# Another order for the first phase of a layer-norm, block-sparse and LoRA gate kernel: two tiles transposed ahead of the first product

## The chip, the cores and the metric

The kernel runs on one core of a Trainium2 chip. The metric is the device time of one execution in microseconds; the median of three runs is given. Five engines run their own instruction streams: TensorE (PE, matrix products and transposes; its weight loads are listed apart as PEld), VectorE (DVE), ScalarE (ACT), GpSimd (POOL) and SyncE (SP), which here only issues DMAs. The profile is one execution that the hardware profiler recorded.

## The reference

The input x has 2 batches of 1024 tokens with 1024 features. Each token is layer-normed, goes through a block-sparse linear layer (a 32 x 32 block of the weight counts if its mask has a nonzero entry) and through a linear layer with eight low-rank experts, whose mixing coefficients come from the mean token of the batch.

```python
def block_sparse(data, mask, weight, bias):
    bm = mask.reshape(Nb, 32, Kb, 32).sum(axis=(1, 3)) > 0
    wb = weight.reshape(Nb, 32, Kb, 32) * bm[:, None, :, None]
    return jnp.einsum('bsk,nk->bsn', data, wb.reshape(N, K)) + bias

def lora(x, W_org, lora_down, lora_up, lora_keys, Wq):
    base = jnp.einsum('bsi,oi->bso', x, W_org)
    q = jnp.einsum('bi,ki->bk', x.mean(axis=1), Wq)
    coeffs = softmax(jnp.einsum('bk,ek->be', q, lora_keys) / sqrt(128))
    h = jnp.einsum('bsi,eir->bser', x, lora_down)
    return base + jnp.einsum('be,bser,ero->bso', coeffs, h, lora_up)

xn = layernorm(x)
out = x + block_sparse(xn, ...) * silu(lora(xn, ...))
```

## The kernel before

Every product of two float32 matrices is made of three products: each factor is split into a high part (a copy rounded to the type that TensorE takes in one pass, written by ScalarE) and a low part (what the rounding left, a subtraction on VectorE or GpSimd), and hi x hi, hi x lo and lo x hi are summed in PSUM. So each tile of weights or of tokens costs one cast and one subtraction, and TensorE waits for both.

The first phase is the block-sparse product of batch 0 (1024 tokens in eight tiles of 128, numbered 0 to 7) with the first 512 output features. Everything from line 652 on is in a written order: TensorE, VectorE, ScalarE and GpSimd each execute their instructions in the order in which the program lists them. SP's order of DMA issues is not written out by hand; the DMAs are issued ahead, as buffers come free.

Tokens come in two ways. Tiles 0 to 3 are loaded as they lie (x_load) and go through x_stats (two halves of batch-norm statistics on VectorE), rstd_of (aggregate and add on VectorE, a power on GpSimd), shift_of (VectorE), x_norm_half (ScalarE, half a tile), x_turn (four 128 x 128 transposes on TensorE for a half), x_hi (ScalarE) and x_lo (VectorE). Tiles 4 to 7 come already transposed from a second copy of x, eight chunks of 128 features: xprep loads a chunk, subtracts the tokens' means (spread over all partitions by spread_means, four transposes on TensorE) and casts it; xprep_lo makes the low part. Their scale is applied when the result is evacuated. Tiles 4 to 7 are also loaded as they lie, because the mean token needs them normed: statistics by x_stats (tiles 4 and 5) or on ScalarE by mean_sum and square_sum with mean_of and rstd_from (6 and 7), then x_norm.

The weights' first 512 columns come in two quarters of 256. For each quarter the mask is summed over its blocks (mask_sum, on VectorE or ScalarE), mask_join and mask_spread make a small matrix of it, mask_apply_mm spreads it with eight small products on TensorE, mask_apply_cp copies it for GpSimd, and w_mul multiplies the weights (VectorE reads the mask in PSUM, GpSimd the copy). w_hi and w_lo split them. The second argument of w_mul, w_hi and w_lo is the first of the chunks of 128 features, two at a time where nothing else is said.

The products: p0 to p3 with t0 to t3 are the first quarter for token tiles 0 to 3, q0 to q3 with u0 to u3 the second quarter, q4 to q7 with u4 to u7 both quarters at once for tiles 4 to 7. t0(2, 4) issues the three products of chunks 2 and 3. PSUM has four banks for them, so q1, q0, q2, q3, and then tiles 4 to 7, need a bank whose former result has been evacuated (quarter_evac, tile_evac, on VectorE).

warm_up(n) issues n products of constants whose result nobody reads. They stand where TensorE would be idle; keep_busy issues some of them inside t0.

The mean token: add_acc adds the normed tiles up in the tile 0 buffer (1024 columns on VectorE or GpSimd); halves splits the sum, query takes its mean over the tokens with four products and multiplies by Wq, scores and soft make the coefficients, scale_up scales the up-projection. y_prep loads and splits chunks of the down-projection, and y_mul(0, 0, 0) is the first product of the next phase. The staging buffers of xprep, y_prep and scale_up are six of one pool.

The lines that matter: x_stats 611 (instruction at 150), rstd_of 152, shift_of 161, x_norm_half 644 (168), x_turn 599 (211), x_hi 602, x_lo 605 (607), mask_sum 250, w_mul 584 (588), w_hi 590, w_lo 593 (595), the products 457, 460 and 461, warm_up 672 (674), xprep 225, xprep_lo 235 (238), add_acc 648 (650), halves 333 (338, 339), query 342 (348 to 357), quarter_evac 484 (473), y_prep 405 (412, 413). Line 1394 is the product of the last phase, 1148 of the one before it.

Of the kernel before, what the change touches and what calls it, by code (L numbers as in the profile page):

```python
# [22 lines left out]
NH = 512  # L23
# [5 lines left out]
NWARM2 = 12  # L29
# [3 lines left out]
def kernel(  # L33
# [618 lines left out]
    with tc.manual_schedule(engines={mybir.EngineType.PE, mybir.EngineType.DVE, mybir.EngineType.Activation, mybir.EngineType.Pool}):  # L652
# [25 lines left out]
        warm_up(NWARM)  # L678
        x_stats(0, 0)
        x_stats(0, 1)  # L680
        rstd_of(0)
        shift_of(0)
        x_norm_half(0, 0)
        x_norm_half(0, 1)
        x_turn(0, 0)
        x_turn(0, 1)
        warm_up(NWARM2)
        x_stats(1, 0)
        x_stats(1, 1)
        rstd_of(1)  # L690
        mask_sum(0, 0, mh[0][:, 0, :], nc.vector)
        x_hi(0, 0)
        mask_sum(0, 1, mh[0][:, 1, NH:], nc.scalar, 1)
# [3 lines left out]
        shift_of(1)  # L697
        mask_apply_mm(0)
        warm_up(4)
        x_hi(0, 1)  # L700
        mask_apply_cp(0, 0, 4, nc.scalar.copy)
        w_mul(0, 0, nc.vector, 1)
        w_mul(0, 1, nc.vector, 1)
        w_mul(0, 2, nc.gpsimd)
        w_hi(0, 0, 1)
        w_hi(0, 1, 1)
        x_lo(0, 0)
        x_norm_half(1, 0)
        w_hi(0, 2)
        w_lo(0, 0, nc.vector, 1)  # L710
        w_lo(0, 1, nc.vector, 1)
        p0, t0 = open_gemm(0, 0, s0, 0, NQ)
        p1, t1 = open_gemm(0, 1, s0, 0, NQ)

        keep_busy = lambda kt: warm_up((4, 1, 2, 0)[kt])
        t0(0, 1, keep_busy)
        x_turn(1, 0)
        t0(1, 2, keep_busy)
        x_hi(1, 0)
        mask_apply_cp(0, 4, 8, nc.scalar.copy)  # L720
        w_lo(0, 2)
        t0(2, 4, keep_busy)
        x_lo(1, 0)
        w_mul(0, 4, nc.vector)
        w_mul(0, 6, nc.gpsimd)
        x_norm_half(1, 1)
        w_hi(0, 4)
        t1(0, 3)
        x_turn(1, 1)
        x_lo(0, 1)  # L730
        w_hi(0, 6)
        w_lo(0, 4)
        x_hi(1, 1)
        t1(3, 4)
        t0(4, 6)
        w_lo(0, 6, nc.gpsimd)
        x_stats(2, 0)
        x_stats(2, 1)
        rstd_of(2)
        mask_sum(1, 0, mh[1][:, 0, :], nc.scalar)  # L740
        t0(6, 8)
        x_lo(1, 1)
        shift_of(2)
        x_norm_half(2, 0)
        x_norm_half(2, 1)
        x_stats(3, 0)
        x_stats(3, 1)
        rstd_of(3)
        add_acc(1, nc.gpsimd)
        t1(4, 7)  # L750
        x_turn(2, 0)
        t1(7, 8)
        x_hi(2, 0)
        x_turn(2, 1)
        x_lo(2, 0)
        shift_of(3)
        x_hi(2, 1)
        x_norm_half(3, 0)
        x_norm_half(3, 1)
        x_lo(2, 1)  # L760
        mask_sum(1, 1, mh[1][:, 1, :], nc.vector)
        mask_spread(1)
        p2, t2 = open_gemm(0, 2, s0, 0, NQ)
        t2(0, 4)
        x_turn(3, 0)
        x_hi(3, 0)
        t2(4, 5)
        mask_apply_mm(1)
        mask_apply_cp(1, copy=nc.scalar.copy)
        w_mul(1, 4, nc.gpsimd)  # L770
        w_mul(1, 6, nc.gpsimd)
        x_lo(3, 0)
        x_turn(3, 1)
        t2(5, 8)
        w_mul(1, 0, nc.vector)
        x_hi(3, 1)
        x_lo(3, 1)
        w_hi(1, 0)
        w_mul(1, 2, nc.vector)
        p3, t3 = open_gemm(0, 3, s0, 0, NQ)  # L780
        t3(0, 8)
        w_hi(1, 2)
        w_hi(1, 4)
        w_hi(1, 6)
        w_lo(1, 0)
        quarter_evac(0, 0, p0)
        w_lo(1, 2)
        mean_sum(6)
        mean_sum(7)
        w_lo(1, 4)  # L790
        w_lo(1, 6)
        quarter_evac(1, 0, p1)
        x_stats(4, 0)
        x_stats(4, 1)
        x_stats(5, 0)
        rstd_of(4)
        x_stats(5, 1)
        q0, u0 = open_gemm(0, 0, s0, NQ, NQ)
        u0(0, 8)
        shift_of(4)  # L800
        x_norm(4)
        rstd_of(5)
        mean_of(6)
        mean_of(7)
        q1, u1 = open_gemm(0, 1, s0, NQ, NQ)
        u1(0, 6)
        spread_means(0, 1)
        u1(6, 8)
        quarter_evac(2, 0, p2)
        xprep(0, 1, 0)  # L810
        xprep(0, 1, 1)
        shift_of(5)
        x_norm(5)
        xprep_lo(0, 1, 0)
        quarter_evac(3, 0, p3)
        q2, u2 = open_gemm(0, 2, s0, NQ, NQ)
# [745 lines left out]
```

## Time and profile before

| | |
|---|---|
| three runs | 438.65, 438.69, 438.95 us |
| profiled execution | 439.04 us, of which 437.3 us from the first to the last instruction (the span) |
| granted TensorE clock | 1.000 |
| instructions | 5766 |

Busy time in five stretches of the first 66 us, from the windows of the profile (us, number of instructions in brackets):

```profile
7.66:13.17 5.51, 5.31 (x32) 3.89 (x32) 4.73 (x12) 3.08 (x8) 1.42 (x2) 1.00 1.03 419
13.17:24.17 11.00, 10.65 (x75) 9.46 (x76) 9.28 (x21) 8.49 (x16) 4.58 (x6) 1.00 1.03 409
24.17:35.74 11.57, 11.57 (x105) 11.50 (x104) 10.91 (x25) 7.84 (x14) 4.38 (x5) 1.00 0.92 345
35.74:56.27 20.53, 20.53 (x121) 18.17 (x119) 19.58 (x38) 13.17 (x23) 4.40 (x5) 1.00 0.47 154
56.27:65.61 9.34, 9.34 (x43) 7.73 (x42) 6.72 (x19) 2.42 (x5) 1.66 (x1) 1.00 0.11 30
```

After the window and its length come PE, PEld, DVE, ACT and POOL, then the granted clock of TensorE, the share of the 16 DMA engines that was busy, and GB/s. The stretches are: from the first transposes to the first product; to the point from which TensorE is never idle; to spread_means; to the query; to the first y_mul. The duration of a TensorE product includes its way through the array, so products overlap and a busy share of 1 is not a measure of useful work; the distance of their starts is.

### The profile page before, as it was taken

Reading aid. Unit: us, or ns where it says so; the run is one execution under the profiler, and the core shown is the slowest. Engines: PE = TensorE matmul, PEld = TensorE weight load, DVE = VectorE, ACT = ScalarE, POOL = GpSimd, SP = SyncE. Lnnn points to the kernel's source line nnn. Section 1 sums busy time; section 2 is a strip of 40 time slices with the busy share of each in tenths; the row PEclk is TensorE's granted clock in tenths of the full one; section 3 lists DMA queues with packets and bytes.
Section 4 is the critical chain, followed back from the end, with each engine's and each line's share of the span. In section 5 each row is a group of like instructions: output and inputs, shape, how many; then the busy total and the mean of one; then the engine's idle time right before and its main releaser. Section 6 shows DMA issues by size and latency. Waiting matters only on the chain.

```text
span 437.3 us, 5766 instructions
## 1 busy us (share of the span) xinstructions
PE 429.7 (98%) x2029; PEld 358.0 (82%) x2029; DVE 305.2 (70%) x508; ACT 184.4 (42%) x312; POOL 79.0 (18%) x103
## 2 busy tenths in 40 slices
PE   7999999999999999999999999999999999999996
PEld 5899888888888888888888888788888888888885
DVE  5889977766626769879966968877647385375624
ACT  3787436354731222236334344466335233441510
POOL 3342210002220313134132130010020030002000
PEclk9999999999999999999999999999999999999999
DMA  7994607676896798984699866996282165228003
GB/s 269 413 371 152 216 25 224 234 253 208 263 296 176 244 268 298 315 327 144 191 273 295 254 191 192 348 253 206 58 210 80 48 141 151 93 54 210 26 1 121
DMA packets 44477, 88.48 MB, mean 202 GB/s; under 512 B 4624, under 2 KB 13088, under 8 KB 44448
## 3 DMA queue, kind: packets, MB, share of 16 engines
q1 hardware_dynamic: 28944, 64.77, 43.6%
q0 software_dynamic: 6624, 16.26, 16.0%
q10 hardware_dynamic: 8880, 7.08, 5.0%
q8 instruction: 16, 0.26, 0.2%
q14 instruction: 13, 0.11, 0.1%
HBM read 68.17 MB, written 19.93 MB: 201 GB/s over the span
## 4 chain that ended last, share of the span: by engine, by line
PE 90%; DMA 4%; DVE 2%; ACT 1%; issue 1%; POOL 0%; SPq 0%; DVEq 0%; ACTq 0%
PE acc_ps L1394 25%; PE acc_ps L461 12%; PE acc_ps L457 12%; PE acc_ps L460 12%; PE py L1394 10%; PE psv L1148 5%; PE psw L421 3%; PE psw L422 3%; PE psw L423 3%; PE psw L1148 2%; DMA xs<-xv 1%; DMA misc<-xv 1%; DMA raw<-xv 1%; PE warm L674 1%; DMA acc<-in_x_dram 1%
## 5 line engine op out<-in xcount | busy, mean ns | idle before, releaser
L1394 PE MATMUL acc_ps<-xw,ow 128*128 128x512 f32 (+1 forms) x492 | 112.2, 384 | 0.3 <-DVE xw L1219 0.3
L457 PE MATMUL acc_ps<-slot,xgrp 128*128 128x512 f32 (+1 forms) x288 | 106.5, 370 | 0.1
L1394 PEld LDWEIGHTS acc_ps<-xw,ow 128*128 128x128 f32 x492 | 90.8, 188 | 19.0 <-DVE xw L1219 0.7
L461 PE MATMUL acc_ps<-slot,xgrp 128*128 128x512 f32 (+1 forms) x288 | 105.5, 366 | 0.2 <-DVE xgrp L607 0.2
L460 PE MATMUL acc_ps<-slot,xgrp 128*128 128x512 f32 (+1 forms) x288 | 105.3, 366 | 0.1
L461 PEld LDWEIGHTS acc_ps<-slot,xgrp 128*128 128x128 f32 x288 | 54.3, 188 | 9.6 <-DVE xgrp L607 0.6
L457 PEld LDWEIGHTS acc_ps<-slot,xgrp 128*128 128x128 f32 x288 | 54.3, 188 | 9.3 <-ACT slot L591 0.6
L460 PEld LDWEIGHTS acc_ps<-slot,xgrp 128*128 128x128 f32 x288 | 54.3, 189 | 8.9 <-POOL slot L595 0.3
L1394 PE MATMUL py<-xw,ow 128*128 128x512 f32 x192 | 46.3, 389 | 0.0
L1394 PEld LDWEIGHTS py<-xw,ow 128*128 128x128 f32 x192 | 36.0, 188 | 7.5
L1262 DVE TENSOR_TENSOR ow<-raw,ow 128x1024 fp32r<-128x1024 f32 (+1 forms) x32 | 34.7, 1088 | 9.2 <-ACT ow L1261 9.1
L1261 ACT CAST ow<-raw 128x1024 fp32r<-128x1024 f32 (+1 forms) x32 | 29.5, 941 | 2.5 <-DVE raw L1255 1.5
L509 POOL DMA_DIRECT2D stash<-in_x_dram x16 | 14.4, 902 | 72.4 <-DVE stash L506 72.4
L1377 POOL DMA_DIRECT2D gate<-in_xT_dram x12 | 10.5, 913 | 93.1 <-DVE gate L1371 67.8
L431 ACT CAST slot<-wo 128x512 fp32r<-128x512 f32 x16 | 9.9, 620 | 35.7 <-DVE wo L428 35.7
L421 PE MATMUL psw<-cut,dhi 128*128 128x512 f32 x64 | 24.9, 389 | 0.0
L422 PE MATMUL psw<-cut,dhi 128*128 128x512 f32 x64 | 24.9, 389 | 0.0
L423 PE MATMUL psw<-cut,dlo 128*128 128x512 f32 x64 | 24.9, 389 | 0.0
L1438 DVE TENSOR_TENSOR py<-py,s 128x512 f32<-128x512 f32 x8 | 5.6, 698 | 27.6 <-ACT s L1401 27.6
L1255 DVE TENSOR_TENSOR raw<-raw 128x512 f32<-128x512 f32 x32 | 21.4, 688 | 0.6
L1247 DVE TENSOR_TENSOR raw<-raw,m_sb 128x1024 f32<-128x1024 f32 x8 | 9.7, 1222 | 13.8 <-DMA raw<-in_wu_dram 13.8
L506 DVE TENSOR_TENSOR stash<-stash,mine 128x512 f32<-128x512 f32 x16 | 11.1, 692 | 10.8 <-ACT mine L482 10.6
(211 smaller groups left out, 604.6 us busy)
## 6 DMA issues: line engine op xcount, KB each, us to landing
wo<-in_worgT_dram SPq DMA_DIRECT2D x24, 256.0 KB, 3.8
raw<-in_x_dram SPq DMA_DIRECT2D x11, 512.0 KB, 4.7
ds<-in_down_dram SPq DMA_DIRECT2D x16, 256.0 KB, 3.1
stash<-in_x_dram POOLq DMA_DIRECT2D x16, 256.0 KB, 5.2
raw<-in_wu_dram SPq DMA_DIRECT2D x8, 512.0 KB, 5.4
raw<-yu SPq DMA_DIRECT2D x8, 512.0 KB, 3.7
out_dram<-stash ACTq DMA_DIRECT2D x14, 256.0 KB, 4.3
misc<-xv SPq DMA_DIRECT2D x12, 256.0 KB, 3.9
```

What stands on the lines that cost most here:

```text
L421: nc.tensor.matmul(ps, lhsT=dhi[:, c, :], rhs=u[c][:, 0, :], start=c == 0, stop=False)
L422: nc.tensor.matmul(ps, lhsT=dhi[:, c, :], rhs=u[c][:, 1, :], start=False, stop=False)
L423: nc.tensor.matmul(ps, lhsT=dlo[:, c, :], rhs=u[c][:, 0, :], start=False, stop=c == 3)
L457: nc.tensor.matmul(ps, lhsT=xs[:, kt, 0, cols], rhs=w[:, kt, 0, wc], start=kt == 0, stop=False)
L460: nc.tensor.matmul(ps, lhsT=xs[:, kt, 0, cols], rhs=w[:, kt, 1, wc], start=False, stop=False)
L461: nc.tensor.matmul(ps, lhsT=xs[:, kt, 1, cols], rhs=w[:, kt, 0, wc], start=False, stop=kt == NKT - 1)
L509: nc.gpsimd.dma_start(res, x[at], accum_op=ALU.add)
L1148: nc.tensor.matmul(ps, lhsT=w[:, a, wl, c, :], rhs=u[:, ul, :], start=start and c == 0 and n == 0, stop=c == 1 and n == 2, skip_group_chec ...
L1255: nc.vector.tensor_tensor(raw[:, o], raw[:, a], raw[:, b], op)
L1261: nc.scalar.copy(o[:, a:b, 0], raw[:, a:b])
L1262: nc.vector.tensor_tensor(o[:, a:b, 1], raw[:, a:b], o[:, a:b, 0].bitcast(F32), ALU.subtract)
L1394: nc.tensor.matmul(ps, lhsT=o[:, a, wl, j, :], rhs=xw[j][:, m, xl, cols], start=start and j == 0 and k == 0, stop=j == 3 and k == 2, skip_ ...
```

## The change

The order of the calls between the first warm_up and the loop of y_mul is another one; the functions that they call are the same. In the main:

- x_norm_half(0, 1) comes before x_norm_half(0, 0). x_turn(0, 0) and x_turn(0, 1) have warm_up(10) between them; before, they stood together with warm_up(12) after them. warm_up(4) after the mask products becomes warm_up(7), and the warm-ups inside t0 go from 4, 1 and 2 to 0, 0 and 2 (32 in all, before 36).
- x_turn(1, 0) comes before the first product t0(0, 1); x_hi(0, 1) and x_lo(0, 1) move behind w_hi(0, 6) and w_lo(0, 4).
- w_mul(0, 4) moves ahead of the low parts of the first chunks, both mask copies ahead of the first w_mul, and the statistics of tile 2 and of tiles 4 and 5 come earlier among VectorE's work. add_acc(1) on GpSimd moves ahead of w_mul(1, 4); mean_sum(7) and mean_of move behind quarter_evac(0, 0).
- u1(0, 6) runs before u0, u6(0, 4) and u5 before u4, and u7 before the last part of u6. spread_means stands after u0.
- The chunks of xprep come in the order 1, 0, 3, 5, 2, 4, 7, 6.
- add_acc(3) and add_acc(4) move up among the evacuations and xprep; before, tiles 2 to 7 were added in one row. y_prep(0, 0, 0) moves ahead of x_norm(5), before the sums are complete; tile_evac of q4, q5 and q6 moves behind scale_up.

The core of the diff:

```diff
         warm_up(NWARM)
+        keep_busy = lambda kt: warm_up((0, 0, 0, 2)[kt])
+        halves, query, scores, soft = coeffs(0)
+
         x_stats(0, 0)
+        p1, t1 = open_gemm(0, 1, s0, 0, NQ)
         x_stats(0, 1)
         rstd_of(0)
         shift_of(0)
+        x_norm_half(0, 1)
         x_norm_half(0, 0)
-        x_norm_half(0, 1)
         x_turn(0, 0)
+        x_hi(0, 0)
+        x_stats(1, 1)
+        x_stats(1, 0)
+        rstd_of(1)
+        mask_sum(0, 1, mh[0][:, 1, NH:], nc.scalar, 1)
+        mask_sum(0, 0, mh[0][:, 0, :], nc.vector)
+        warm_up(10)
         x_turn(0, 1)
-        warm_up(NWARM2)
-        x_stats(1, 0)
-        x_stats(1, 1)
-        rstd_of(1)
-        mask_sum(0, 0, mh[0][:, 0, :], nc.vector)
-        x_hi(0, 0)
-        mask_sum(0, 1, mh[0][:, 1, NH:], nc.scalar, 1)
+        p0, t0 = open_gemm(0, 0, s0, 0, NQ)
+        shift_of(1)
         mask_sum(0, 1, mh[0][:, 1, :NH], nc.vector)
         mask_join(0)
         mask_spread(0)
-        shift_of(1)
+        x_norm_half(1, 0)
         mask_apply_mm(0)
-        warm_up(4)
-        x_hi(0, 1)
         mask_apply_cp(0, 0, 4, nc.scalar.copy)
+        x_lo(0, 0)
+        mask_apply_cp(0, 4, 8, nc.scalar.copy)
         w_mul(0, 0, nc.vector, 1)
+        warm_up(7)
         w_mul(0, 1, nc.vector, 1)
+        w_mul(0, 4, nc.vector)
+        w_hi(0, 0, 1)
+        w_lo(0, 0, nc.vector, 1)
+        x_turn(1, 0)
+        w_hi(0, 1, 1)
+        w_lo(0, 1, nc.vector, 1)
+        t0(0, 1)
         w_mul(0, 2, nc.gpsimd)
-        w_hi(0, 0, 1)
-        w_hi(0, 1, 1)
-        x_lo(0, 0)
-        x_norm_half(1, 0)
         w_hi(0, 2)
-        w_lo(0, 0, nc.vector, 1)
-        w_lo(0, 1, nc.vector, 1)
-        p0, t0 = open_gemm(0, 0, s0, 0, NQ)
-        p1, t1 = open_gemm(0, 1, s0, 0, NQ)
-
-        keep_busy = lambda kt: warm_up((4, 1, 2, 0)[kt])
-        t0(0, 1, keep_busy)
-        x_turn(1, 0)
-        t0(1, 2, keep_busy)
-        x_hi(1, 0)
-        mask_apply_cp(0, 4, 8, nc.scalar.copy)
         w_lo(0, 2)
-        t0(2, 4, keep_busy)
-        x_lo(1, 0)
-        w_mul(0, 4, nc.vector)
         w_mul(0, 6, nc.gpsimd)
         x_norm_half(1, 1)
+        x_stats(2, 0)
+        x_stats(2, 1)
+        x_hi(1, 0)
+        x_lo(1, 0)
+        p2, t2 = open_gemm(0, 2, s0, 0, NQ)
+        rstd_of(2)
         w_hi(0, 4)
+        w_lo(0, 4)
+        w_hi(0, 6)
+        x_hi(0, 1)
+        x_lo(0, 1)
+        t0(1, 2)
+        t0(2, 4, keep_busy)
+        x_turn(1, 1)
+        x_hi(1, 1)
         t1(0, 3)
-        x_turn(1, 1)
-        x_lo(0, 1)
-        w_hi(0, 6)
-        w_lo(0, 4)
-        x_hi(1, 1)
         t1(3, 4)
+        shift_of(2)
+        mask_sum(1, 0, mh[1][:, 0, :], nc.scalar)
         t0(4, 6)
         w_lo(0, 6, nc.gpsimd)
-        x_stats(2, 0)
-        x_stats(2, 1)
-        rstd_of(2)
-        mask_sum(1, 0, mh[1][:, 0, :], nc.scalar)
-        t0(6, 8)
         x_lo(1, 1)
-        shift_of(2)
+        t1(4, 7)
         x_norm_half(2, 0)
+        x_turn(2, 0)
         x_norm_half(2, 1)
+        x_hi(2, 0)
         x_stats(3, 0)
         x_stats(3, 1)
         rstd_of(3)
-        add_acc(1, nc.gpsimd)
-        t1(4, 7)
-        x_turn(2, 0)
+        x_turn(2, 1)
         t1(7, 8)
-        x_hi(2, 0)
-        x_turn(2, 1)
+        x_hi(2, 1)
         x_lo(2, 0)
         shift_of(3)
-        x_hi(2, 1)
         x_norm_half(3, 0)
         x_norm_half(3, 1)
-        x_lo(2, 1)
+        t0(6, 8)
+        t2(0, 4)
+        x_turn(3, 0)
         mask_sum(1, 1, mh[1][:, 1, :], nc.vector)
         mask_spread(1)
-        p2, t2 = open_gemm(0, 2, s0, 0, NQ)
-        t2(0, 4)
-        x_turn(3, 0)
+        mask_apply_mm(1)
+        x_stats(4, 0)
+        x_lo(2, 1)
         x_hi(3, 0)
-        t2(4, 5)
-        mask_apply_mm(1)
+        x_lo(3, 0)
         mask_apply_cp(1, copy=nc.scalar.copy)
+        x_turn(3, 1)
+        x_hi(3, 1)
+        add_acc(1, nc.gpsimd)
+        quarter_evac(1, 0, p1)
+        w_mul(1, 2, nc.vector)
+        w_mul(1, 0, nc.vector)
+        w_hi(1, 0)
         w_mul(1, 4, nc.gpsimd)
         w_mul(1, 6, nc.gpsimd)
-        x_lo(3, 0)
-        x_turn(3, 1)
+        x_lo(3, 1)
+        x_stats(5, 1)
+        w_lo(1, 0)
+        w_hi(1, 2)
+        w_lo(1, 2)
+        w_hi(1, 4)
+        w_lo(1, 4)
+        w_hi(1, 6)
+        t2(4, 5)
         t2(5, 8)
-        w_mul(1, 0, nc.vector)
-        x_hi(3, 1)
-        x_lo(3, 1)
-        w_hi(1, 0)
-        w_mul(1, 2, nc.vector)
+        mean_sum(6)
         p3, t3 = open_gemm(0, 3, s0, 0, NQ)
         t3(0, 8)
-        w_hi(1, 2)
-        w_hi(1, 4)
-        w_hi(1, 6)
-        w_lo(1, 0)
+        q1, u1 = open_gemm(0, 1, s0, NQ, NQ)
+        w_lo(1, 6)
+        u1(0, 6)
         quarter_evac(0, 0, p0)
-        w_lo(1, 2)
-        mean_sum(6)
+        x_stats(5, 0)
+        rstd_of(5)
+        quarter_evac(2, 0, p2)
         mean_sum(7)
-        w_lo(1, 4)
-        w_lo(1, 6)
-        quarter_evac(1, 0, p1)
-        x_stats(4, 0)
+        mean_of(7)
+        mean_of(6)
+        square_sum(6, 0)
+        q0, u0 = open_gemm(0, 0, s0, NQ, NQ)
         x_stats(4, 1)
-        x_stats(5, 0)
+        q2, u2 = open_gemm(0, 2, s0, NQ, NQ)
         rstd_of(4)
-        x_stats(5, 1)
-        q0, u0 = open_gemm(0, 0, s0, NQ, NQ)
         u0(0, 8)
+        add_acc(3, nc.vector)
         shift_of(4)
+        quarter_evac(3, 0, p3)
+        q3, u3 = open_gemm(0, 3, s0, NQ, NQ)
+        spread_means(0, 1)
+        xprep(0, 1, 1)
+        u1(6, 8)
+        quarter_evac(1, 1, q1)
+        xprep(0, 1, 0)
+        xprep(0, 1, 3)
+        xprep_lo(0, 1, 3, nc.gpsimd)
+        square_sum(6, 1)
+        xprep_lo(0, 1, 1, nc.vector)
+        square_sum(7, 0)
+        xprep(0, 1, 5)
+        u2(0, 8)
+        xprep_lo(0, 1, 0)
+        xprep(0, 1, 2)
+        rstd_from(6)
+        square_sum(7, 1)
         x_norm(4)
-        rstd_of(5)
-        mean_of(6)
-        mean_of(7)
-        q1, u1 = open_gemm(0, 1, s0, NQ, NQ)
-        u1(0, 6)
-        spread_means(0, 1)
-        u1(6, 8)
-        quarter_evac(2, 0, p2)
-        xprep(0, 1, 0)
-        xprep(0, 1, 1)
+        quarter_evac(0, 1, q0)
+        xprep(0, 1, 4)
+        q6, u6 = open_gemm(0, 6, s0)
+        xprep_lo(0, 1, 2, nc.vector)
+        shift_of(6)
+        quarter_evac(2, 1, q2)
+        xprep(0, 1, 7)
         shift_of(5)
+        rstd_from(7)
+        xprep(0, 1, 6)
+        q4, u4 = open_gemm(0, 4, s0)
+        xprep_lo(0, 1, 6)
+        u3(0, 8)
+        u6(0, 4)
+        xprep_lo(0, 1, 4, nc.vector)
+        add_acc(4, nc.vector)
+        shift_of(7)
+        y_prep(0, 0, 0)
+        q5, u5 = open_gemm(0, 5, s0)
         x_norm(5)
-        xprep_lo(0, 1, 0)
-        quarter_evac(3, 0, p3)
-        q2, u2 = open_gemm(0, 2, s0, NQ, NQ)
-        u2(0, 8)
-        q3, u3 = open_gemm(0, 3, s0, NQ, NQ)
-        u3(0, 8)
-        for kt in range(2, 6):
-            xprep(0, 1, kt)
-            xprep_lo(0, 1, kt - 1, nc.gpsimd if kt == 4 else nc.vector)
-            if kt == 3:
-                quarter_evac(0, 1, q0)
-            square_sum(6 + (kt - 2) // 2, kt % 2)
-        xprep(0, 1, 6)
         xprep_lo(0, 1, 5, nc.gpsimd)
-        xprep(0, 1, 7)
-        rstd_from(6)
-        rstd_from(7)
-        xprep_lo(0, 1, 6)
         xprep_lo(0, 1, 7)
-        quarter_evac(1, 1, q1)
-        q4, u4 = open_gemm(0, 4, s0)
+        u5(0, 8)
+        add_acc(2, nc.vector)
+        quarter_evac(3, 1, q3)
         u4(0, 8)
-        shift_of(6)
-        shift_of(7)
+        x_norm(7)
         x_norm(6)
-        x_norm(7)
-        for i in range(2, 6):
-            add_acc(i, nc.vector)
-        quarter_evac(2, 1, q2)
+        add_acc(5, nc.vector)
         add_acc(6, nc.vector)
-        quarter_evac(3, 1, q3)
-        for h in range(2):
-            add_acc(7, nc.vector, h)
-        halves, query, scores, soft = coeffs(0)
+        add_acc(7, nc.vector, 0)
+        add_acc(7, nc.vector, 1)
         halves()
-        y00 = new_slot()
-        q5, u5 = open_gemm(0, 5, s0)
-        u5(0, 8)
-        q6, u6 = open_gemm(0, 6, s0)
-        u6(0, 4)
         query()
-        tile_evac("s", 0, 0, 4, q4)
-        y_prep(0, 0, 0)
         u6(4, 7)
+        q7, u7 = open_gemm(0, 7, s0)
         scores()
-        tile_evac("s", 0, 0, 5, q5)
         soft()
         scale_up(0, 0)
-        y_prep(0, 0, 1)
+        tile_evac("s", 0, 0, 4, q4)
+        u7(0, 8)
         u6(7, 8)
         tile_evac("s", 0, 0, 6, q6)
-        q7, u7 = open_gemm(0, 7, s0)
-        u7(0, 8)
+        y_prep(0, 0, 1)
+        tile_evac("s", 0, 0, 5, q5)
+        y00 = new_slot()
         for k in range(NKT):
             y_mul(0, 0, k)
             if k == 0:
```

More of the change, by code (lines that the diff above doesn't have):

```diff
@@ L28 @@
 NWARM = 13
-NWARM2 = 12
 @with_exitstack
```

## The prediction

> **What bounds the kernel now.** I read first the page's busy shares and the chain that ended last, then the waits of TensorE.
>
> ```profile
> PE 429.7 (98%) x2029; PEld 358.0 (82%) x2029; DVE 305.2 (70%) x508; ACT 184.4 (42%) x312; POOL 79.0 (18%) x103
> PE 90%; DMA 4%; DVE 2%; ACT 1%; issue 1%; POOL 0%; SPq 0%; DVEq 0%; ACTq 0%
> PE pt L211 <- ACT acc L168: 1.5, 1, 1.5
> PE warm L674 <- DVE ones_r L98: 1.1, 1, 1.1
> PE acc_ps L1394 <- DVE xw L1219: 0.3, 1, 0.3
> PE acc_ps L461 <- DVE xgrp L607: 0.2, 1, 0.2
> ```
>
> TensorE is the bound: after 24.17 us it waits once, 0.3 us, late in the kernel. So a microsecond won before the first y_mul product (65.61) should reach the end, as all later work hangs on TensorE's progress. The timeline of TensorE shows what can be won: matmuls without a use, and gaps.
>
> ```profile
> 1.12 4.98 PE L674 MATMUL warm<-ones_r 128*128 128x512 f32 x13 [1.12 <-DVE ones_r L98]
> 7.66 1.36 PE L211 MATMUL pt<-ident,acc 128*128 128x128 f32 x8 [1.55 <-ACT acc L168]
> 8.77 2.99 PE L674 MATMUL warm<-ones_r 128*128 128x512 f32 x12
> 11.66 0.34 PE L276 MATMUL mp<-r,misc 128*128 128x8 bf16 x8
> 11.86 1.16 PE L674 MATMUL warm<-ones_r 128*128 128x512 f32 x4
> 13.17 0.39 PE L457 MATMUL acc_ps<-slot,xgrp 128*128 128x256 f32 x1
> 13.39 1.08 PE L674 MATMUL warm<-ones_r 128*128 128x512 f32 x4
> 23.94 0.39 PE L461 MATMUL acc_ps<-slot,xgrp 128*128 128x256 f32 x1 [0.22 <-DVE xgrp L607]
> 56.27 0.39 PE L348 MATMUL mxp<-mh,inv_s 128*128 128x512 f32 x1
> ```
>
> Columns: start, time, engine, line, operation. The last line, the first query product, is my mark: both orders have issued the same useful products by then (u4, u5, half of u6 and all quarters). From 7.66 to 56.27 are 48.61 us. Starts lie 0.227 apart for a product of 512 columns, 0.1195 for 256, and about 0.38 cover a group of four transposes. Useful: 60 x 0.227 + 192 x 0.1195 + 8 x 0.38 + 0.35 (means) + 0.42 (16 mask products) = 40.4. The remaining 8.2 are 23 warm-ups (5.2) and 3.0 of gaps.
>
> The second engine is VectorE, strictly in order: it ends the last part of halves() only here.
>
> ```profile
> 11.44 0.17 DVE L266 SCALAR_TENSOR_TENSOR r<-s,pick 128x8 bf16<-128x8 f32 x1
> 12.26 0.75 DVE L588 TENSOR_TENSOR ramp<-ramp,mp 128x256 f32<-128x256 f32 x2 [0.52 <-ACT m_sb L283]
> 36.37 1.28 DVE L231 TENSOR_TENSOR xt<-xt,mean_ps 128x512 f32<-128x512 f32 x2 [0.60 <-PE mean_ps L221]
> 55.26 1.30 DVE L339 TENSOR_TENSOR ml<-acc,mh 128x512 fp32r<-128x512 f32 x2
> ```
>
> Between 11.44 and 56.56 its gaps of over 0.3 are 0.52, 0.43, 0.40, 0.60, 0.49 and 0.60: 3.04. It has little more to give than TensorE, so both chains must be worked through.
>
> **The change, step by step.** Starts on VectorE lie 0.60 apart for 512 columns, 0.33 for 256, 1.23 for a sum of 1024; ScalarE's 512-column casts 0.55 to 0.60; all from the timelines.
>
> *Start.* The halves of tile 0 are normed in the other order, so the first transposes wait for the second norm: 8.36, where before the second group stood. That is 0.70 later, hidden: ten warm-ups follow (8.78 to 11.05), then the other four transposes, and TensorE next needs the mask. On VectorE shift_of(1) (0.13) now stands ahead of the second mask sum, so the spread ends at 11.75 and the mask products start at 11.74 (before 11.60 by the weight load).
>
> *To the first product.* Both mask copies now precede the weights' multiply. Before, w_mul waited for the copy's end (12.23), not for TensorE's (12.00); so I let it wait for the second copy: 12.18 + 0.10 + 0.19 = 12.47, w_mul at 12.50 (12.40 if it waits for the first only). Then VectorE runs without a break: two w_mul (0.33 each), the w_mul of tiles 4 and 5 moved here (0.60), w_lo(0) to 14.18, w_lo(1) to 14.51, w_lo(2,3) to 15.10, two statistics of tile 2 (1.2), x_lo(1,0) 16.2 to 16.9, aggregate 0.32, w_lo(4,5) to 17.8, x_lo(0,1) to 18.43, x_lo(1,1) to 19.16. What it asks of the DMAs has landed, by issue plus landing time of the DMA view: w tiles 4 to 7 at 12.85 (asked 13.16), x2 14.1 (15.0), x3 17.9 (19.1), x4 23.1 (23.5), x5 24.4 (27.4). The queue's order at the start is unchanged.
>
> *TensorE.* Seven warm-ups end at 13.67, the transposes of tile 1 at 14.08: first product there, 0.9 later than before, but with tile 1's half ready and little left to wait for: w_lo(0) to 14.22, w_lo(2,3) to 15.14; two warm-ups in kt 3 (0.45); transposes 16.2; t1 waits for x_lo(1,0) to 16.95 (0.11); t0(4) and t1(4) for x_lo(0,1) and x_lo(1,1) (0.1 each). t1(4,7) ends at 20.04, where ScalarE has just normed tile 2 (19.5 and 20.3, behind its mask sum), and t0 and t1 are complete at 21.95 with both transposes of tile 2 done. Before, they were complete at 22.73 with one transpose group to go: 1.2 ahead. The gap at 23.94 goes too: x_lo(2,0) is done at 22.0, as t2 starts. t2(4) waits 0.14 for x_lo(2,1), which now stands behind the statistics of tile 4.
>
> *Second quarter.* t3 ends at 28.9; u1 needs w_lo(1,0) (28.7), w_lo(1,4) (29.9); u0 needs the bank that quarter_evac(0,0) frees (30.87, against 31.07). So u1(0,6) before u0 covers the evacuation. The transposed means start at 33.94, same set as before at 35.74: 1.8 ahead. Moved ScalarE sums (mean_sum 6 and 7, 29.2 to 31.5) are in time for them.
>
> *GpSimd and SP.* GpSimd: w_mul(0,2) and (0,6) 12.5 to 14.6 (cast at 16.0), w_lo(0,6) 17.8 to 19.1 (product 19.8), add_acc(1) 21.2 to 23.6, now ahead of its w_mul(1,4), which waits for the second mask's copy (24.7) anyway. SP: the raw load that waits for add_acc(1) goes 2 us earlier, the one behind add_acc(2) 1 us later (49.4); ScalarE reads the first from 72.5 on, which covers both.
>
> *Second group.* u1 rest, u2, u3, half of u6, u5, u4 run on: 0.72 + 2 x 2.87 + 12 x 0.227 + 2 x 5.44 + 0.35 = 20.4, giving 54.36. Checked on the way: lo(2) 41.5 against its product at 42.6; lo(4) 45.6 against 46.6; lo(7) 48.2 against 48.7. VectorE waits here 0.75 for the cast of tile 6, which stands behind x_norm(4) on ScalarE (44.3). y_prep(0,0,0) is moved ahead of the sums: 0.60 for dlo on VectorE, one cast on ScalarE, and two DMAs on SP's queue behind the last two xT loads; the first freed staging buffer (xprep_lo(3) on GpSimd, 39.3) lets ds land at 39.3 + 2.9 = 42.2, cast at 44.3 to 44.9, no wait. Then from 48.2 four sums (4.92), one eviction (0.33), ScalarE's hi (0.12 of waiting) and two lo (1.30): 54.87. The fourth query product is due at 55.04. Fits, by 0.17 only.
>
> *Last part.* After the query: u6(4,7), scores, 27 products, as before, so y_mul starts at 65.61 - 1.91 = 63.7. The softmax chain loses two operations between its steps (an evacuation and dlo), so the cuts come 2.4 earlier. In exchange three evacuations follow the cuts: dlo(1) ends at 66.3 against its product at 66.8, and the second psw bank's sum ends at 68.4 against 69.1. Both hold.
>
> **Sum.** At the mark: 56.27 - 54.36 = 1.91. By parts: four warm-ups less 0.9, gaps 3.0 less about 1.3, minus 0.70 for the later start. The profiled execution took 439.04 (span 437.3, 1.74 around it): 437.1. The median is 0.35 below that execution: 438.69 - 1.9 = 436.8. Bounds of what the trace doesn't show: w_mul behind one copy instead of two gains 0.1; the gaps in their new places could all close, 1.3 by TensorE, but VectorE allows 0.17 there plus its own 1.35 of waits, so gain at most 2.6; at the other end VectorE's waits stay at 3.04 as now, its last lo at 56.5 then, gain 0.4. I take the worked value.
>
> The trace's clock row: the first eight warm-ups start 0.45 apart, those from 8.77 on 0.227, after a stretch (6.10 to 8.77) that held only eight transposes. The new order has the same stretch, 6.10 to 8.78, with four. [...]
>
> **Rivals.**
> 1. *VectorE takes over the bound* (a wait in place of those removed). For: 0.17 of margin at the query, gaps of about 1 us in the 33 before it, and strict order, so ds landing late stops lo(7) and all sums. If ds got the buffer of kt 5 (free 45.2) it would land at 48.1, dlo 1.85 late. Against: buffers freed earlier exist. Gain 0 to 0.8, time 438.3.
> 2. *Given back later*: the chain shows DMA from 262 to 283 (misc and xs from xv). Were those loads bound by something fixed, the end would stay at 438.7. Against: all their sources and buffers hang on earlier products, and TensorE waits 0.3 there.
> 3. *Slower: the clock.* The array falls to half rate at 8.78 and stays there through both warm-up strings. Ten at 0.45 put the mask products at 13.7 (+1.95); alone that takes the gain away. It decides from the point where the seven run slowly too: +1.5 more, 1.5 slower than now, 440.2. Against: the equal stretch before.
>
> **Chances.** Forecast (gain 0.9 to 2.6) 0.76; rival 1 0.13; rival 2 0.05; rival 3 0.04, other losses beyond 0.9 us 0.02. Within 0.2% (0.88 us) is what a measurement cannot tell from none. Faster 0.76, same 0.18, slower 0.06. Range 436.0 to 438.4: from the upper bound of the gain to rival 1's time.
>
> **What would show it.** Right: first t0 product near 14.1, means' transposes near 33.9, first query product near 54.4, y_mul near 63.7, and from there the old timeline 1.9 earlier. Wrong: warm-ups from 8.8 on spaced 0.45; a wait of TensorE on L339 or L238; dlo (L413) waiting for ds before 50 us; y_mul early but the end unmoved.

## The result, and the profile after

The changed kernel takes 440.4 us in the median of 22 runs (438.78 to 441.88). The kernel before took 438.85 in the same measurement (22 runs, 437.92 to 440.81). The ratio on record, taken over all runs and not from the two medians, is 1.0026, with a 95% interval of [1.0014, 1.0038]: slower by a quarter of a per cent, where 0.4% less was predicted. The profiled execution took 440.35 us, its span 438.6, and its mean granted TensorE clock was 0.996 (before: 439.04, 437.3, 1.000).

The busy shares, the chain that ended last, all that the first 70 us hold of TensorE's own waits, and the two waits of its weight loads (PEld) that matter below, after the change (after a wait: us in total, times, the longest):

```profile
PE 430.9 (98%) x2025; PEld 358.6 (82%) x2025; DVE 306.2 (70%) x508; ACT 183.8 (42%) x312; POOL 79.6 (18%) x103
PE 91%; DVE 6%; ACT 1%; DMA 1%; issue 1%; POOL 0%; SPq 0%
PE pt L210 <- ACT acc L167: 1.9, 1, 1.9
PE warm L673 <- DVE ones_r L97: 1.1, 1, 1.1
PE acc_ps L459 <- DVE slot L594: 0.4, 1, 0.4
PEld acc_ps L460 <- DVE xgrp L237: 1.3, 3, 0.5
PEld mxp L348 <- DVE ml L338: 0.6, 2, 0.3
```

Four instructions fewer on TensorE, yet 1.2 us more of busy time, and 1.0 more on VectorE for the same 508 instructions. The same work lasted longer. The chain has gone from 2% to 6% VectorE: TensorE now waits for it, for low parts of weights (slot) and tokens (xgrp) and for the low part of the mean token (ml). Before, no weight load had waited between 24.2 us and the first y_mul. TensorE's timeline (start, time, engine, line, operation; line numbers of this phase are one lower than before):

```profile
1.12 5.53 PE L673 MATMUL warm<-ones_r 128*128 128x512 f32 x13 [1.12 <-DVE ones_r L97]
8.50 0.63 PE L210 MATMUL pt<-ident,acc 128*128 128x128 f32 x4 [1.85 <-ACT acc L167]
8.88 4.12 PE L673 MATMUL warm<-ones_r 128*128 128x512 f32 x10
12.80 0.64 PE L210 MATMUL pt<-ident,acc 128*128 128x128 f32 x4
13.27 0.34 PE L275 MATMUL mp<-r,misc 128*128 128x8 bf16 x8
15.53 0.36 PE L456 MATMUL acc_ps<-slot,xgrp 128*128 128x256 f32 x1
16.31 0.39 PE L459 MATMUL acc_ps<-slot,xgrp 128*128 128x256 f32 x1 [0.42 <-DVE slot L594]
57.79 0.39 PE L347 MATMUL mxp<-mh,inv_s 128*128 128x512 f32 x1
```

The ten warm-ups hold the array for 3.92 us, from 8.88 to 12.80, where 2.27 was predicted. The mask products start at 13.27 instead of 11.74; the first product has 0.78 to the second. The query is at 57.79, predicted 54.36. In the same four stretches, from the windows (after the window and its length: PE, PEld, DVE, ACT, POOL, granted clock, DMA share, GB/s):

```profile
8.50:15.53 7.03, 7.03 (x38) 5.72 (x38) 5.97 (x14) 3.40 (x9) 2.17 (x3) 0.76 1.03 418
15.53:36.33 20.80, 20.36 (x172) 19.69 (x171) 19.88 (x44) 14.92 (x28) 8.61 (x9) 1.00 0.95 349
36.33:57.79 21.46, 21.26 (x120) 17.93 (x119) 19.98 (x37) 13.17 (x21) 4.68 (x5) 1.00 0.49 163
57.79:67.49 9.70, 9.70 (x43) 7.58 (x42) 5.84 (x17) 2.80 (x6) 1.65 (x1) 1.00 0.01 3
```

The first line carries a granted clock of 0.76, and VectorE is busy for 19.88 of the second's 20.80 us. Put beside the prediction, by the distances between marks in TensorE's timeline:

| stretch, us | predicted | before | after | after less predicted |
|---|---|---|---|---|
| start of the mask products | 11.74 | 11.66 | 13.27 | 1.53 |
| to spread_means | 22.20 | 24.08 | 23.06 | 0.86 |
| to the query | 20.42 | 20.53 | 21.46 | 1.04 |
| to y_mul | 9.34 | 9.34 | 9.70 | 0.36 |
| start of y_mul | 63.70 | 65.61 | 67.49 | 3.79 |

From y_mul to the end of the span are 371.1 us (before 371.7): the rest of the kernel follows y_mul. The whole question lies in 3.79 us of the first 67.

**Two causes in the trace.** (A third, a load that landed later than in the trace of before, stands under the mis-sized term below.) The first is the clock. TensorE's windows of the warm-ups alone (PE, PEld, granted clock, DMA share, GB/s):

```profile
9.00:9.50 0.50, 0.50 (x3) 0.42 (x4) 0.95 1.06 434
9.50:12.50 3.00, 3.00 (x9) 2.20 (x7) 0.50 1.02 419
12.50:13.00 0.50, 0.50 (x2) 0.00 (x0) 0.64 0.98 401
```

Half rate (a granted clock of 0.50) holds from about 9.45 to 12.86, some 3.4 us. It follows a stretch without warm-ups from 6.65 to 8.88 that held four transposes. The drop comes after the hole, with warm-ups already running again since 8.88.

The second is VectorE. Lines of VectorE's and of GpSimd's timeline after the change:

```profile
15.23 1.03 DVE L594 TENSOR_TENSOR slot<-ramp,slot 128x256 fp32r<-128x256 f32 x1
25.41 0.45 DVE L265 SCALAR_TENSOR_TENSOR r<-s,pick 128x8 bf16<-128x8 f32 x1
41.23 1.40 DVE L237 TENSOR_TENSOR xgrp<-xt,xgrp 128x512 fp32r<-128x512 f32 x1
```

```profile
13.92 2.06 POOL L587 TENSOR_TENSOR ramp<-ramp,m_sb 128x512 f32<-128x512 f32 x2 [3.08 <-ACT m_sb L282]
23.42 2.41 POOL L649 TENSOR_TENSOR acc<-acc,raw 128x1024 f32<-128x1024 f32 x1
35.90 1.46 POOL L157 TENSOR_TENSOR rstd<-ve,mhalf 128x1 f32<-128x1 f32 x1 [1.12 <-DVE ve L156]
40.79 1.29 POOL L237 TENSOR_TENSOR xgrp<-xt,xgrp 128x512 fp32r<-128x512 f32 x1 [3.43 <-ACT xgrp L231]
```

Elsewhere in the same trace w_lo of 256 columns takes 0.42, the spread's line 0.17, xprep_lo 0.68 and the power 0.55. Each long one stands beside an operation of the other engine and ends 0.03 to 0.55 us after it: w_lo(0, 0) at 16.26 after GpSimd's multiplies at 15.98, the spread at 25.86 after add_acc at 25.83, xprep_lo(0) at 42.63 beside GpSimd's to 42.08, and the power at 37.36 behind VectorE's add_acc(3), which runs from 35.73 to 36.94. Operations of VectorE that read PSUM, statistics and reductions kept their durations beside GpSimd in this trace: an x_lo took 0.69 (at 23.44) and a mask sum 1.21 (at 24.17) beside add_acc, and two halves of statistics took 1.28 at 21.12, where GpSimd's w_lo(0, 6) ran to 21.55, against 1.27 at 17.12 beside nothing. So the trace has it in both directions, on operations with two inputs in SBUF; "blocked" stands below for such a longer duration, and what makes it is not shown.

### The profile page after: what moved, and what is told of

Same layout as the page of the kernel before. It is cut to its first block, busy times and chain, and to the rows that moved or that the text cites. A ratio compares the mean times of both kernels' runs of the same rounds, so it can differ in the third digit from the quotient of the medians.

```text
span 438.6 us, 5757 instructions
## 1 busy us (share of the span) xinstructions
PE 430.9 (98%) x2025; PEld 358.6 (82%) x2025; DVE 306.2 (70%) x508; ACT 183.8 (42%) x312; POOL 79.6 (18%) x103
## 3 DMA queue, kind: packets, MB, share of 16 engines
q0 software_dynamic: 6624, 16.26, 15.7%
## 4 chain that ended last, share of the span: by engine, by line
PE 91%; DVE 6%; ACT 1%; DMA 1%; issue 1%; POOL 0%; SPq 0%
PE acc_ps L1402 25%; PE acc_ps L460 12%; PE acc_ps L459 12%; PE acc_ps L456 12%; PE py L1402 10%; PE psv L1156 6%; PE psw L421 3%; PE psw L422 3%; PE psw L420 3%; PE psw L1156 2%; DVE xt L230 1%; PE warm L673 1%; DVE xgrp L237 1%; DMA acc<-in_x_dram 1%; DVE slot L594 1%; PE pt L210 1%
```

## The experiments

Each batch ran on a chip of its own and shares the runs of the kernel before there: 439.12 us in the first (e1 to e4), 438.97 in the second (e5 to e8), 438.89 in the third (e9 to e11). Ratios are to these, and across batches the ratios are compared.

**e1: the clock alone.** Seven more warm-ups fill the hole before the first transposes.

```diff
-NWARM = 13
+NWARM = 20
```

> The changed kernel with 20 instead of 13 warm-ups at the very start, so that TensorE is busy up to about 8.3 us. Clock theory: the granted clock of 0.50 between 10 and 12 us in the changed kernel comes from the hole 6.65 to 8.50; with it filled, the ten warm-ups after the first transposes start 0.227 apart, the mask products stand near 12.6 instead of 13.27 (VectorE's spread ends at 12.52), the low-clock runs become rare and the median falls from 440.4 by 0.7 to 1.7, to about 439. Rival, that only VectorE's blocked instructions count: the median stays at 440.4 within 0.3.

439.5 us (438.63 to 441.8, 12 runs), ratio 1.0006 [0.9988, 1.0025]. TensorE's timeline of e1:

```profile
8.81 2.55 PE L673 MATMUL warm<-ones_r 128*128 128x512 f32 x10
12.16 0.34 PE L275 MATMUL mp<-r,misc 128*128 128x8 bf16 x8 [0.36 <-DVE r L265]
15.20 0.39 PE L459 MATMUL acc_ps<-slot,xgrp 128*128 128x256 f32 x1 [0.42 <-DVE slot L594]
```

Full rate throughout, and the mask products 1.11 earlier. The wait of 0.42 for w_lo stands as before, so it doesn't come from the clock; the later stretches are those of the changed kernel (23.06 and 21.47).

**e2: GpSimd's work elsewhere.** Nothing is left out; three places of VectorE's and GpSimd's order change so that the longest of those operations with two SBUF inputs no longer meet ("..." marks lines left out).

```diff
         x_lo(0, 0)
-        mask_apply_cp(0, 4, 8, nc.scalar.copy)
...
-        w_mul(0, 6, nc.gpsimd)
...
         x_hi(1, 0)
+        mask_apply_cp(0, 4, 8, nc.scalar.copy)
         x_lo(1, 0)
+        w_mul(0, 6, nc.gpsimd)
         p2, t2 = open_gemm(0, 2, s0, 0, NQ)
...
+        x_hi(0, 1)
         w_hi(0, 6)
-        x_hi(0, 1)
...
         add_acc(3, nc.vector)
-        shift_of(4)
...
         xprep(0, 1, 3)
+        shift_of(4)
...
-        xprep_lo(0, 1, 0)
...
         quarter_evac(0, 1, q0)
+        xprep_lo(0, 1, 0)
```

> The changed kernel with three places reordered so that VectorE's operations on two SBUF operands don't stand beside GpSimd's: the second mask copy and GpSimd's w_mul(0,6) later, shift_of(4) behind three xprep, xprep_lo(0) behind xprep(2). Theory of blocking: in the changed kernel w_lo(0,0) took 1.03 instead of 0.42, xprep_lo(0) 1.40 instead of 0.68, and the power for tile 4 1.46 instead of 0.55; without these 0.6 + 0.7 + 0.4 = 1.7 VectorE ends the last part of halves that much earlier and the median falls from 440.4 to about 438.7, at the same share of low-clock runs. Rival, that only the clock counts: 440.4 stays.

438.39 us (437.25 to 439.87, 12 runs), ratio 0.9976 [0.9958, 0.9993]. VectorE's timeline of e2:

```profile
13.85 1.35 DVE L594 TENSOR_TENSOR slot<-ramp,slot 128x256 fp32r<-128x256 f32 x3
24.60 0.69 DVE L149 BATCH_NORM_STATS2 st<-xlate 128x6 f32<-128x512 f32 x1 [0.72 <-DMA xlate<-in_x_dram]
```

Three w_lo now take 1.35 together, where after the change they took 1.97. What was won there is lost again at tile 4: its load landed at 24.6 (23.1 was predicted), VectorE stood 0.72 for it, and TensorE then waited 0.83 for the x_lo behind it, so that the stretch to spread_means is 23.16, no shorter than after the change. What e2 wins it wins in the stretch to the query, 20.53. The power still took 1.46, with nobody waiting for it. TensorE's timeline of e2 adds a fact on the clock:

```profile
8.36 0.63 PE L210 MATMUL pt<-ident,acc 128*128 128x128 f32 x4 [2.58 <-ACT acc L167]
8.74 2.54 PE L673 MATMUL warm<-ones_r 128*128 128x512 f32 x10
```

It idled 2.58 us, longer than the 1.85 of the result's profile, and the ten warm-ups ran at full rate all the same. The length of the hole alone doesn't decide.

**e3 and e4: the start by itself.** e3 puts the old start into the changed kernel, e4 the new start into the kernel before (its edit here):

```diff
-        x_norm_half(0, 0)
         x_norm_half(0, 1)
+        x_norm_half(0, 0)
         x_turn(0, 0)
+        warm_up(10)
         x_turn(0, 1)
-        warm_up(NWARM2)
```

> The changed kernel with the start of the kernel before: first half of tile 0 normed first, both transpose groups together, twelve warm-ups behind them. Clock theory: low-clock runs as rare as before the change, median about 438.9 to 439.2. Rival, that the later landing of tile 1 (8.49 instead of 7.70) comes from ScalarE's table load, which stood at 4.83 instead of 3.60: with the old order of the halves the load is back at 3.60 and tile 1 lands at 7.7; if the landing is a matter of the single execution, it falls anywhere between 7.7 and 8.5 whatever the order. Only blocking counts: 440.4 stays.

> The kernel before with the new start alone: halves of tile 0 normed in the other order, ten warm-ups between the two transpose groups, none behind them. Clock theory: the granted clock falls to 0.50 around 10 to 12 us in most runs, and the median rises from 438.85 by 1 to 1.7, to about 440.2. Rival, that the start is harmless and all of the loss lies later: 438.9 within 0.4.

e3: 439.86 us (438.68 to 441.69, 12 runs), 1.0006 [0.9986, 1.0025]. e4: 439.65 (438.31 to 443.36, 12 runs), 1.0015 [0.9989, 1.0041]. Both lie between the two kernels, with intervals that overlap those of both: the medians settle nothing on the start, and e3's is above what was expected of it. TensorE's timeline of e3 shows why:

```profile
9.47 4.51 PE L673 MATMUL warm<-ones_r 128*128 128x512 f32 x12
```

Twelve warm-ups in 4.51: the old start can meet half rate too. And the profiled execution of e4, with the new start, had none. So the drop comes in some executions of either order, and had to be counted (below).

**e5 to e8: the two cures together.** e5 is the changed kernel again, unaltered. e6 joins e1's edit and e2's. e7 adds to e6 that the statistics of tile 4 no longer stand where a late load stops VectorE, and that the second group's low parts are ordered so that VectorE's no longer stand behind GpSimd's (the edit beyond e6's):

```diff
-        x_stats(4, 0)
         x_lo(2, 1)
+        quarter_evac(1, 0, p1)
+        x_stats(4, 0)
...
-        quarter_evac(1, 0, p1)
...
-        x_norm(4)
...
         q6, u6 = open_gemm(0, 6, s0)
-        xprep_lo(0, 1, 2, nc.vector)
-        shift_of(6)
+        xprep_lo(0, 1, 5, nc.gpsimd)
         quarter_evac(2, 1, q2)
         xprep(0, 1, 7)
+        shift_of(6)
+        xprep_lo(0, 1, 2, nc.vector)
...
         q4, u4 = open_gemm(0, 4, s0)
+        x_norm(4)
+        xprep_lo(0, 1, 4, nc.vector)
...
         u6(0, 4)
-        xprep_lo(0, 1, 4, nc.vector)
+        xprep_lo(0, 1, 7)
...
-        xprep_lo(0, 1, 5, nc.gpsimd)
-        xprep_lo(0, 1, 7)
```

e8 is the kernel before with `NWARM = 20`.

> The changed kernel unaltered, beside the three next ones on one chip, as their reference. If low-clock runs (a mean granted clock of 0.996 or less) are a matter of chance from one execution to the next, their share and so the median move: between 439.2 and 440.6, and the fastest run near 438.8 as on record. If they belong to this order, their share is again near one half and the median near 440.4.

> The changed kernel with the hole filled (20 warm-ups at the start) and with the three places reordered where VectorE stood beside GpSimd. If the two causes are separate and add, the median is 1.0 to 1.9 below that of the hole filled alone (439.5), about 438.0, and no run has a mean clock of 0.996 or less. If they are one (whichever is taken away, the other sets the time), it stays near the 438.4 of the reordering alone.

> As the one before, and two more waits of VectorE taken away that remain in the profile of the reordered kernel: the statistics of tile 4 behind two other operations (there VectorE waited 0.72 for the tile's DMA, and TensorE 1.0 for x_lo(2,1) behind it), and GpSimd's xprep_lo(5) ahead of the power for tile 7 with x_norm(4) behind the casts (there 0.69 of waiting for the cast of tile 6 and 0.4 of a blocked xprep_lo(6)). If VectorE's chain sets the query, 0.7 to 1.5 less than the kernel with both, about 437.0; if TensorE's own products set it by now, less than 0.4 comes of it.

> The kernel before with 20 instead of 13 warm-ups at the start, nothing else. Clock theory: its few runs of 440.5 and more go, the fastest and the median hardly move (median lower by 0 to 0.4). If the hole has no part in those runs, they stay: about one run in six above 440.4.

| | median (lowest to highest, runs) | ratio to before |
|---|---|---|
| e5 | 439.47 (438.71 to 443.78, 12) | 1.0021 [0.9999, 1.0043] |
| e6 | 437.54 (437.18 to 439.59, 11) | 0.9976 [0.996, 0.9991] |
| e7 | 437.35 (436.85 to 437.92, 10) | 0.9954 [0.9939, 0.9969] |
| e8 | 438.85 (438.38 to 439.81, 11) | 0.9995 [0.9983, 1.0008] |

e7 is faster than both kernels. Its page and TensorE's timeline:

```profile
PE 429.7 (99%) x2032; PEld 358.4 (82%) x2032; DVE 304.6 (70%) x508; ACT 183.9 (42%) x312; POOL 80.5 (18%) x103
```

```profile
8.15 0.63 PE L210 MATMUL pt<-ident,acc 128*128 128x128 f32 x4 [0.50 <-ACT acc L167]
8.53 2.56 PE L673 MATMUL warm<-ones_r 128*128 128x512 f32 x10
11.91 0.34 PE L275 MATMUL mp<-r,misc 128*128 128x8 bf16 x8 [0.39 <-DVE r L265]
54.73 0.39 PE L347 MATMUL mxp<-mh,inv_s 128*128 128x512 f32 x1
```

VectorE is busy for 1.6 us less than in the changed kernel, with the same 508 instructions. The stretches of e7 are 22.19, 20.63 and 9.35 us, against 22.20, 20.42 and 9.34 predicted: without half rate, and with most of the blocks that TensorE waited for out of the way, the predicted chain is nearly what the chip runs. Blocks that nobody waits for are still in it: the power for tile 4 takes 1.46, the spread 0.44. Beside e6, e7's median is 0.19 lower where 0.7 to 1.5 was expected, though its y_mul starts 0.86 earlier in the profiles (64.08 against 64.94). Whether the two cures add isn't settled: e6 fell 1.96 below e1 in the median, as two separate causes would have it, but its ratio is that of e2 alone, 0.9976. e8 says that filling the hole is worth nothing in the median to the kernel before, whose drops are rare; e5 that the changed kernel without a drop in its profile starts the mask products at 11.94, and is still no faster than before.

**e9 to e11: which place is worth what.** All three with `NWARM = 20`. e9 has e2's first place (the second mask copy and w_mul(0, 6) later), e10 its other two, e11 the first place and tile 4's statistics behind the evacuation, as in e7.

> The hole filled and only the first of the three places reordered (second mask copy and GpSimd's w_mul(0,6) later, so that VectorE's w_lo(0,0) no longer takes 1.03). From the mask products to the transposed means the profiles with and without this place show the same 23.05 us (11.94 to 34.99 and 11.96 to 35.01). If the 0.6 is absorbed by the wait for tile 4's DMA (0.61 to 0.72 in the reordered kernels), the stretch stays at 23.0 to 23.1 and the median at that of the unaltered kernel, about 439.4. If it is worth its 0.6 by itself, the stretch is near 22.4 and the median near 438.8.

> The hole filled and only the two later places reordered (shift_of(4) behind three xprep, xprep_lo(0) behind xprep(2)). From the transposed means to the query the changed kernel took 21.46 and 21.49 us, with the places reordered 20.53. If these two places alone are the loss there, the stretch is again 20.5 and the median 0.9 or more below the unaltered kernel's, 438.0 to 438.6.

> The hole filled, the first place reordered, and the statistics of tile 4 moved behind x_lo(2,1) and an evacuation. If the two losses stand behind each other on VectorE, both together give what neither gives alone: mask products to transposed means 22.2 (as in the kernel with everything, 22.19) and not 23.05; means to query still 21.4, so that part of the gain is kept and the median is 438.3 to 438.8. If the first place has no part in it, moving the statistics alone accounts for less than 0.7 of the stretch and it stays above 22.6.

| | median (lowest to highest, runs) | ratio to before | to spread_means | to the query |
|---|---|---|---|---|
| e9 | 438.83 (438.27 to 440.13, 12) | 0.9999 [0.9986, 1.0011] | 22.35 | 21.50 |
| e10 | 438.07 (437.7 to 440.33, 12) | 0.9986 [0.9975, 0.9997] | 23.06 | 20.53 |
| e11 | 438.73 (438.18 to 439.64, 11) | 0.9991 [0.9978, 1.0005] | 22.20 | 21.64 |

Each place shortens its own stretch: the early one takes 0.71 from e1's 23.06 (0.86 with tile 4 out of the way), the late ones 0.94 from its 21.47. The other stretch stays as it was within 0.03, except that e11 gives 0.17 back in its second. In e2, which has the late places too, no weight load waits for a low part of the tokens in the second stretch any more, where after the change three did (1.3 in all). e10's profiled execution kept the gain to y_mul (64.93) and still had a span of 438.6: some 2 us were lost far behind this phase, where TensorE waited 0.8 and 0.5 us for dw and xw. No other profile shows that, and the median doesn't carry it; what it was stays open.

**The clock, counted.** Every run lists its mean granted clock. One stretch of 3.41 us at half rate takes 0.004 off the mean of 437 us (0.5 x 3.41 / 437). At or below 0.996 were:

| kernels | executions |
|---|---|
| new start, hole open (after, e2, e4, e5) | 19 of 58 (11 of 22, 3 of 12, 4 of 12, 1 of 12) |
| old start, hole open (before in the three batches, e3) | 8 of 110 |
| hole filled (e1, e6 to e11) | 0 of 79 |

The 58 and the 110 are pooled over four measurements, and the share of the same changed kernel was 11 of 22 in one and 1 of 12 in another.

The six profiles with the hole open (before, after, e2 to e5) point to what decides. In each, the first warm-ups start 0.43 apart up to a moment and 0.23 from it on: at 4.88, 6.04, 4.16, 5.88, 5.16 and 6.47 us. In the two with a drop, half rate began 3.41 behind that moment (at 9.45 after the change, at 9.29 in e3). These are the windows of the warm-ups alone over the 3.41 us behind it (PE, PEld, granted clock, DMA share, GB/s), of before, after, e2, e3, e4 and e5 in this order:

```profile
4.88:8.29 3.41, 1.23 (x6) 0.66 (x4) 1.00 0.93 336
6.04:9.45 3.41, 1.18 (x6) 0.68 (x5) 1.00 0.99 390
4.16:7.57 3.41, 1.61 (x7) 0.96 (x6) 1.00 0.93 284
5.88:9.29 3.41, 0.68 (x3) 0.20 (x2) 1.00 1.01 399
5.16:8.57 3.41, 1.32 (x6) 0.81 (x5) 1.00 0.98 321
6.47:9.88 3.41, 1.70 (x8) 1.15 (x7) 1.00 1.02 405
```

Warm-ups ran for 1.18 (after) and 0.68 us (e3) in the two with a drop, and for 1.23, 1.61, 1.32 and 1.70 us in the other four. So the place of the hole behind that moment sorts all six, and its length doesn't: e3 and e4 both idled 1.71, one with a drop and one without. With the transposes counted in they don't sort either (1.56 and 1.66 with a drop, 1.61 and 1.70 in e2 and e4 without). This is read from six profiles, with 0.05 us between the two sets; no run moved the hole to test it.

In the 22 runs of the result, the eleven at or below 0.996 took 440.0 to 441.3 us, and the five at 438.78 to 439.21 all had 0.999 or more. Six of 440.1 to 441.9 at 0.998 to 1.000 remain unexplained.

## Why the prediction was wrong

**What held.** TensorE's useful work and its spacing, the order of the two groups, the copy that w_mul waits for, and the statement that what is won before y_mul reaches the end. Rival 2 (given back later) falls, by 371.1 to 372.1 us from y_mul to the end in every profile but e10's. The predicted y_mul at 63.7 is met by e7 within 0.4 (64.08).

**The step that failed first: "To the first product", "Then VectorE runs without a break", and with it "Second group".** VectorE's operations were laid end to end at the durations of the trace of before, while GpSimd was planned beside them with its own. The step took the two engines as independent. Here they were not. In the second row of the table (0.86 over the prediction) w_lo(0, 0) lost 0.61, and e9 took 0.71 off the stretch by that place alone; the rest went in e11 with tile 4's statistics, while the spread was still blocked there (0.41), so its 0.28 isn't shown to have cost anything. In the third row (1.04) VectorE stood 0.44 before shift_of(4) for the blocked power, lost 0.72 in xprep_lo(0) and about 0.4 in xprep_lo(6), and three weight loads of TensorE then waited for low parts (0.26, 0.51 and 0.54). e10 took the first two away by order alone and the stretch fell to 20.53; in e6, which has the same two places, xprep_lo(6) and the one behind it still took 1.76, as after the change. In the fourth row (0.36) two weight loads waited for ml, which VectorE's lateness had pushed back. The trace of before could have told it. Its groups of GpSimd, shapes kept apart, have the same power at two durations:

```profile
L158 POOL TENSOR_TENSOR rstd<-ve,mhalf 128x1 f32<-128x1 f32 x6 | 3.3, 554 | 12.5 <-DVE ve L157 11.8 <-DVE mean L620 0.6
L639 POOL TENSOR_TENSOR rstd<-ve,mhalf 128x1 f32<-128x1 f32 x2 | 1.6, 829 | 0.0
```

829 ns against 554 for one operation of one shape: the two took 1022 and 636, and the first started at 45.38, while VectorE ran two xprep_lo from 45.30 to 46.59. VectorE itself showed nothing: in the old order GpSimd's add_acc(1) (23.20 to 25.59) stood beside two x_lo and a mask sum on VectorE (0.69 and 1.21), its multiplies (26.74 to 28.80) beside x_lo and w_mul (0.68 to 0.69), its two xprep_lo (from 41.54 and 44.13) mostly beside xprep (0.68), and VectorE's longest xprep_lo was 0.69.

**The step that failed second: "hidden" in Start, and the clock paragraph.** The later first transposes were called free, as ten warm-ups follow, and the stretch without warm-ups was found equal to the old one. In the result's profiled execution it was even shorter (2.23 us against 2.68) and yet the array went to half rate for 3.4 us: 1.65 on the ten warm-ups, of which about 0.70 reached the mask products (below). Rival 3 had this drop and the price of its first half (1.95), but gave it 0.04, the equal stretch being its only reason, an estimate from the one execution of before; the seven later warm-ups ran at full rate (1.86 us), so its second half didn't come. A third of the new start's executions pay it, against 7% of the old. How much of the median it takes depends on the share: 11 of 22 in the result, 1 of 12 in e5. It isn't the larger cause: e1, with no such drop in any run, stands at 1.0006 where the forecast was 0.9957 (436.8 to 438.69), and that distance was closed by removing the blocks and the late load's wait (e7, 0.9954).

**Rival 1** named VectorE, and one of the prediction's signs of being wrong came, TensorE's waits for the low parts (lines 237 and 338 now), but for another reason. ds landed in time and dlo ran without a wait; the margin of 0.17 at the query was gone because of the blocks ahead of it.

**A term that was mis-sized.** Landings were taken from one execution as fixed. Tile 1's raw load was there by 6.26 in e4's profile and landed at 7.70 in that of before and at 8.49 in the result's. Tile 4's landed at 23.1 in that of before; in e6 and e2 VectorE waited for it to 24.46 and 24.60. In the result's profile the late tile 1 put the end of VectorE's spread at 12.52. In e1 and e7 the mask products start 0.05 behind that end, so here they could have started at about 12.57 (an estimate) even at full rate: of the first row's 1.53, some 0.83 is this load and 0.70 the clock. In e2 tile 4's landing cost 0.7 of VectorE's time right behind the place where a block had been removed.

**A bound that does not follow.** The upper end of the gain, 2.6, is not what its terms give: the worked 1.91 and the 1.3 of gaps that it lets TensorE close make 3.2, and VectorE's 0.17 and 1.35 would allow them. The result lies on the other side, so nothing hung on it.

## What to carry to other kernels

When work is reordered on VectorE and GpSimd, lay the two timelines side by side and mark every operation with two SBUF inputs: in the four pairs read above from the trace after the change one of the two took 0.28 to 0.91 us longer. So put GpSimd's long ones beside VectorE's reads of PSUM, its statistics and its reductions, which kept their times there (0.69, 1.28 for two, 1.21). Fill a stretch in which TensorE waits for something else anyway: it cost nothing here (e8, ratio 0.9995), while an open one is paid for in some executions only (27 of 168 at or below a clock of 0.996, filled 0 of 79), which a single profile can't show, so count the granted clock over all runs. A place in an engine's strict order that reads a fresh load needs a margin for the spread of its landing (here from 6.26 or before to 8.49 us), not for one landing.

## What the runs showed of the hardware that I had not expected

- Operations with two fp32 inputs in SBUF that took longer where VectorE and GpSimd both ran one: 0.42 became 1.03, 0.68 became 1.40, 0.17 became 0.45 on VectorE, and 0.55 became 1.46 on GpSimd.
- A stretch of 2.23 us without warm-ups, 1.85 of it idle and the rest four transposes, was followed by 3.4 us at half rate (a granted clock of 0.50); in e2 2.58 us of idling were followed by ten warm-ups in 2.54, at full rate. Where the hole lies in the 3.41 us behind the first change of rate sorts the six profiles that had it open (warm-ups for 1.18 and 0.68 us with a drop, 1.23 to 1.70 without); that is read from the traces and was not tried.
- The same 512 KB load, issued at 1.71 us in the profiles of before and after, landed at 7.70 and at 8.49 us there, and was there by 6.26 in e4. I had blamed ScalarE's table load for the late one; e3 had that load back in its old place, at 3.48, and tile 1 still landed at 7.87, so that explanation falls and the cause is open.
